# Moving the head transposes of two self-attention blocks into the logits' PSUM slots, and loading weight chunks two ahead

## The chip, the cores and the metric

The kernel runs on one core of a Trainium2 chip. The metric is device time in microseconds (us) of one launch. The kernel before takes 5064.57 us (median of 3 runs, 5062.13 to 5067.9).

## The reference, cut to what matters

A residual stream `x` of 4 batches x 1024 tokens x 288 channels goes through four blocks: a quantised transformer block (0), a cross-attention block (1), a fake-quantised transformer block (2) and a second quantised transformer block (3). The change touches the self-attention of blocks 0 and 3, and the weight preparation that runs beside it:

```python
def quant_linear(q, s, qsum, w, b):        # one scale and zero point per output row of w
    wmax, wmin = jnp.max(w, axis=1), jnp.min(w, axis=1)
    sw = (wmax - wmin) / 255.0 + 1e-08
    zw = _ste_round(-wmin / sw) - 128.0
    qw = jnp.clip(_ste_round(w / sw[:, None]) + zw[:, None], -128.0, 127.0)
    ...
# self-attention: 16 heads of 18 channels, 1024 queries x 1024 keys per batch
logits = jnp.einsum('bqhd,bkhd->bhqk', q, k) / sqrt(18)
o = jnp.einsum('bhqk,bkhd->bqhd', softmax(logits), v)
```

## The kernel before, in words

`quant_net` runs a quantised block: first `quant_self` (self-attention), then cross-attention and the feed-forward part. `quant_self` is called for block 0 (about 55 to 850 us of the profile) and for block 3 (about 3820 to 4600 us); both run the same code.

**The attention loop.** It goes over 4 batches `b`, 4 groups `g` of 4 heads, 2 halves `qh` of 512 queries, and 8 key tiles `kt` of 128 keys: 256 steps a block. A step issues, in program order:

1. logits: two PSUM tiles from `ps2()`, each two banks wide; four matmuls at L2021, one per head, each on its own 32 rows of the array. Heads 0 and 1 write one tile, heads 2 and 3 the other; below these are the two *pairs* of logits. Each matmul is fp32 and appears as two records, so a whole step's logits are "x8" and one pair is "x4";
2. two exponentials on ScalarE (L2031), one per pair, into buffers `e` of the pool `ep`;
3. `weigh` for the step *before*: four matmuls (L1981) that add exp(logits) times values into the accumulator `acc`, a tile from `ps1()`. At the last key tile VectorE copies `acc` to `oT` (L1992). At `kt == 1` of the next head group `turn_heads` calls `heads_done`: four transposes of `oT` on TensorE (L1936), then on VectorE a reciprocal (L1942), a product into the attention output `a` (L1943) and two small reductions (L1953, L1954);
4. `step()`: one piece of side work, if there is any. The list `side` holds the projections of the next group (`operands`, L1896), the next batch's norms and quantisation (`levels`, L1434 and L2358), its values (`values`, L277) and the output projection (`output`, L277). When the list is empty, one piece of `spare` is taken.

**PSUM.** `psum_attn` gives 3 slots of two banks to `ps2()` and 2 slots of one bank to `ps1()`[...]. `acc` holds one `ps1` slot nearly always; the other is shared by every piece of side work and by `heads_done`.

**The order.** Semaphores, slots and each engine's instruction order are set at compile time by a list scheduler: it follows program order as priority, but an engine whose next instruction has no free slot or no data yet, by the scheduler's own estimate, gets a later one that has. [...]

**The weight preparation.** `spare` runs `ctx_aside` and then `ff_aside`, which prepares the two feed-forward weights through `level_pieces`. That loads a chunk of 1152 numbers per partition by a DMA from SyncE's queue (L1545, 432 KB) into a buffer `wn`, reduces it to maxima and minima on VectorE (L1558, L1559), turns these into scales (tile `wps`, 2 buffers), quantises it in 12 pieces (L1583, L1584, L1589), transposes each piece on TensorE (L1599), copies it (L1610) and stores it (L1611). Each of the two feed-forward weights has three chunks, so there are six chunk loads a block. The other weights fit in one chunk each. `wn` has two buffers, and the load of the next chunk is issued when work on a chunk begins.

Of the kernel before, what the change touches and what calls it, by code (L numbers as in the profile page):

```python
# [28 lines left out]
F32 = mybir.dt.float32  # L29
# [7 lines left out]
P = 128  # L37
# [1141 lines left out]
class Fast(Net):  # L1179
# [344 lines left out]
    def level_pieces(self, np_, wd, n_in, width, p, put, sw, bias=None):  # L1524

        nc = self.nc
        oc = wd.shape[0] // p  # L1530
        extra = 0 if bias is None else N_TERMS
        kc = (n_in + extra) // width
        per = max(1, 1152 // n_in)
        run = 3
        if extra:
            bt = np_.tile([p, oc], F32, name="wbias")
            nc.sync.dma_start(bt, bias.rearrange("(c p) -> p c", p=p))
            terms = np_.tile([p, 4, N_TERMS], BF16, name="wterms")
        src = wd.rearrange("(c p) i -> p c i", p=p)

        def load(c0):
            m = min(per, oc - c0)
            wn = np_.tile([P, 1152], F32, tag="wn", name="wn", bufs=2)
            wn = wn[:p, : m * n_in].rearrange("p (c i) -> p c i", c=m)
            nc.sync.dma_start(wn, src[:, c0 : c0 + m, :])  # L1545
            return m, wn

        first = load(0)
        yield
        yield  # L1550
        for c0 in range(0, oc, per):
            m, wn = first
            if c0 + per < oc:
                first = load(c0 + per)
            st = self.sm.tile([P, 6, 4], F32, tag="wps", name="wps", bufs=2)
            mx, mn, rsw, lo, hi = (st[:p, k, :m] for k in range(5))
            s = sw[:, c0 : c0 + m]
            nc.vector.tensor_reduce(mx, wn, AX.X, ALU.max)  # L1558
            nc.vector.tensor_reduce(mn, wn, AX.X, ALU.min)  # L1559
            nc.vector.tensor_tensor(s, mx, mn, ALU.subtract)  # L1560
            nc.vector.tensor_scalar(s, s, 1.0 / 255.0, 1e-8, ALU.mult, ALU.add)
            nc.vector.reciprocal(rsw, s)
            nc.vector.tensor_tensor(lo, mn, rsw, ALU.mult)
            nc.vector.tensor_scalar(lo, lo, -1.0, MAGIC, ALU.mult, ALU.add)
            nc.vector.tensor_scalar(lo, lo, MAGIC, -1.0, ALU.subtract, ALU.mult)
            nc.vector.tensor_scalar(hi, lo, 255.0, None, ALU.add)
            self.watch_range(-256.0, 1.0, lo, "wext")
            if extra:
                d = st[:p, 5, :m]
                nc.gpsimd.tensor_tensor(d, bt[:, c0 : c0 + m], rsw, ALU.mult)  # L1570
                self.three_parts(d, [terms[:, :m, k : k + 1] for k in range(3)])
                for k, n in ((3, 0), (4, 1), (5, 0)):
                    nc.gpsimd.tensor_copy(terms[:, :m, k], terms[:, :m, n])
            yield
            runs = [(c, k0) for c in range(m) for k0 in range(0, kc, run)]
            ahead = None

            for n in range(len(runs) + 1):
                now = ahead
                if n < len(runs):  # L1580
                    c, k0 = runs[n]
                    t = wn[:, c, k0 * width : min((k0 + run) * width, n_in)]
                    nc.vector.tensor_scalar(t, t, rsw[:, c : c + 1], MAGIC, ALU.mult, ALU.add)  # L1583
                    nc.vector.tensor_scalar(  # L1584
                        t, t, MAGIC, lo[:, c : c + 1], ALU.subtract, ALU.max
                    )
                    q = np_.tile([P, run * P], BF16, tag="pq", name="q", bufs=2)
                    q = q[:p, : run * width]
                    nc.vector.tensor_scalar(  # L1589
                        q[:, : run * width - extra], t, hi[:, c : c + 1], None, ALU.min  # L1590
                    )
                    if extra:
                        nc.gpsimd.tensor_copy(q[:, run * width - extra :], terms[:, c, :])
                    ahead = (q, c, k0)
                if now:
                    q, c, k0 = now
                    ps = self.ps1(BF16)
                    for k in range(run):
                        nc.tensor.transpose(  # L1599
                            ps[:width, k * p : (k + 1) * p],  # L1600
                            q[:, k * width : (k + 1) * width],
                            self.idb[:p, :p],
                        )
                    ps = ps[:width, : run * p].rearrange("p (k o) -> p k o", o=p)
                    dst, stored = put(c0 + c)
                    dst = dst[:, k0 : k0 + run, :]
                    if stored:
                        to = np_.tile([P, run * P], BF16, tag="to", name="to", bufs=2)
                        to = to[:width, : run * p].rearrange("p (k o) -> p k o", o=p)
                        nc.vector.tensor_copy(to, ps)  # L1610
                        nc.sync.dma_start(dst, to)  # L1611
                    else:
                        nc.vector.tensor_copy(dst, ps)
                    yield
# [9 lines left out]
    def ctx_aside(self, w, ctxT, mask, cw, np_):  # L1624
# [8 lines left out]
        for b in range(B):  # L1633
            m = np_.tile([P, NTB * T], F32, tag="kv", name="msk")
# [14 lines left out]
        nc.sync.dma_start(cw["swo"].rearrange("(c p) -> p c", p=CK), swo)  # L1649
        kb = cw["kb"]  # L1650
        for g in range(NG):
            wk = np_.tile([P, 1152], F32, tag="wn", name="wn", bufs=2)
            wk = wk[:CK, : NC3 * P].rearrange("p (c o) -> p c o", c=NC3)
            nc.sync.dma_start(
                wk, w["wk2"].rearrange("(c p) o -> p c o", p=CK)[:, :, g * P : (g + 1) * P]
            )
            kg = np_.tile([P, NTB * T], F32, tag="kv", name="kg")
            kg = kg.rearrange("p (b k) -> p b k", b=B)
            nc.gpsimd.memset(kg, 0.0)
            yield  # L1660
            yield
            ps = self.ps1()
            for k in range(NC3):
                nc.tensor.matmul(
                    ps[:, : B * T].rearrange("p (b k) -> p b k", b=B),
                    lhsT=wk[:, k, :],
                    rhs=ctx[:, k, :, 0, :],
                    start=(k == 0),
                    stop=(k == NC3 - 1),
                )  # L1670
            for i in range(4):
                rows = slice(i * HP, (i + 1) * HP)
                nc.vector.tensor_scalar(
                    kg[rows, :, i % 2 * T : (i % 2 + 1) * T],
                    ps[rows, : B * T].rearrange("p (b k) -> p b k", b=B),
                    bk[rows, g : g + 1], None, ALU.add,
                )
            yield

            for pr in range(2):  # L1680
                rows = slice(pr * 64, (pr + 1) * 64)
                ps = self.ps1()
                for b in range(B):
                    nc.tensor.matmul(
                        ps[:, b : b + 1], lhsT=kg[rows, b, :], rhs=bq[rows, g : g + 1],
                        start=True, stop=True,
                    )
                nc.vector.tensor_scalar(
                    kb[:, :, g, pr : pr + 1], ps[:, :B].unsqueeze(2), SCALE, None, ALU.mult
                )  # L1690
                yield
            nc.vector.tensor_scalar(kg, kg, wq["sw"][:, g : g + 1], None, ALU.mult)
            nc.sync.dma_start(cw["kbd"][:, :, g, :], kg)
            yield
        wv = np_.tile([P, 1152], F32, tag="wn", name="wn", bufs=2)
        wv = wv[:CK, : NC3 * C].rearrange("p (c o) -> p c o", c=NC3)
        nc.sync.dma_start(wv, w["wv2"].rearrange("(c p) o -> p c o", p=CK))
        yield
        for b in range(B):
# [4 lines left out]
            ps = self.ps1()  # L1704
# [70 lines left out]
    def quant_self(self, L, w, beside, ready):  # L1775
# [5 lines left out]
        with ExitStack() as es:  # L1781
            pool = lambda name, bufs: es.enter_context(tc.tile_pool(name=name, bufs=bufs))
# [3 lines left out]
            if ready is not None:  # L1786
                wqk = []
                for k in "qk":
                    m = {"T": wp.tile([CK, NC3, NG * P], BF16, name=f"w{k}1T")}
# [6 lines left out]
                wv, wo = (  # L1796
                    self.stored_weight(wp, ready[k], ready[f"s{k}"], w[f"b{k}1"], f"w{k}1")
                    for k in "vo"
                )
            else:  # L1800
                with self.psum8(f"{L}w"), tc.tile_pool(name=f"{L}an", bufs=2) as np_, self.work(f"{L}anw"):
# [7 lines left out]
                        wqk.append(m)  # L1809
                    wv = self.level_weight(wp, np_, [(w["wv1"], w["bv1"])], C, CK, "wv1")  # L1810
                    wo = self.level_weight(wp, np_, [(w["wo1"], w["bo1"])], C, CK, "wo1")
            ep = pool(f"{L}ep", 6)
            es.enter_context(self.work(f"{L}ak"))
            ext = wp.tile([P, 2, 2 * B * NG], F32, name="sext")
            es.enter_context(self.psum_attn(f"{L}x"))
# [115 lines left out]

            def heads_done(b, g, qh, o):

                ps = self.ps1()
                for tt in range(4):
                    nc.tensor.transpose(  # L1936
                        ps[:, tt * P : (tt + 1) * P], o[:, tt * P : (tt + 1) * P], self.idf
# [13 lines left out]
                m = t0 // 4 * NG + g  # L1951
# [1499 lines left out]
```

## Time and profile before

| | |
|---|---|
| median of 3 runs | 5064.57 us |
| span of the profiled execution | 5064.5 us |
| TensorE busy over the span | 4346.0 us (86%) |
| ScalarE busy | 3106.6 us (61%) |
| VectorE busy | 3001.7 us (59%) |
| self-attention loops, TensorE busy | 727.89 of 760 us (block 0), 724.80 of 747 us (block 3) |
| transposes at L1936 | 256, that is 64 groups of four |
| chunk loads at L1545 of feed-forward weights | 12 |

The profile is of one execution. In its timeline a line is: start in us, length in us, engine, line of the kernel, operation, output<-inputs, shapes, number of instructions merged; in brackets the engine's idle time before it and who ended that idle time. "PE" is TensorE's matmuls, "PEld" its weight loads (which overlap matmuls), "DVE" VectorE, "ACT" ScalarE, "POOL" GpSimd, "SPq" SyncE's DMA-issuing queue.

### The profile page before, as it was taken

The page shows a single profiled execution, that of the slowest core. Times are in us where ns is not written, and L with a number is a line of the kernel's source. Part 1 is how long each engine was busy: PE and PEld are TensorE (multiplying, and loading weights), DVE is VectorE, ACT ScalarE, POOL GpSimd, SP SyncE. Part 2 cuts the span into 40 slices and gives each one's busy share as a digit, 9 for nine tenths or more (in the row PEclk, how much of TensorE's full clock was granted, in tenths as well). Part 3 has the DMA queues.
Part 4 walks back from the last instruction along what each step waited for, and adds up shares of the span by engine and source line. Part 5 has one row for each costly group of instructions (what it writes and reads, how often), then busy time and mean ns, then how long its engine had stood idle before and what let it go on. Part 6 is the DMA issues. An engine that isn't in the chain of part 4 may idle for free. (4 is left out here: it accounts for less than half of the span.)

```text
span 5064.5 us, 63950 instructions
## 1 busy us (share of the span) xinstructions
PE 4346.0 (86%) x23291; PEld 1740.0 (34%) x23291; DVE 3001.7 (59%) x6686; ACT 3106.6 (61%) x4374; POOL 1273.7 (25%) x2013
## 2 busy tenths in 40 slices
PE   5999996889898979998798873899998999996786
PEld 2233322545566411100233331455543223322343
DVE  8453253665564679999688778433235444344775
ACT  3776765476663269998788853212215767764796
POOL 1001002442412567200122224111101000003664
PEclk9999997899899955555788785899998999997897
DMA  2000002100001221000000032000000000011000
GB/s 79 3 4 12 7 24 62 60 21 16 1 15 43 112 82 36 11 0 0 23 25 25 22 107 79 23 12 10 1 1 15 7 2 11 15 25 30 16 17 20
DMA packets 135638, 136.00 MB, mean 27 GB/s; under 512 B 69260, under 2 KB 111884, under 8 KB 133648
## 3 DMA queue, kind: packets, MB, share of 16 engines
q1 hardware_dynamic: 134112, 128.13, 8.5%
q0 software_dynamic: 1200, 3.69, 0.3%
q8 instruction: 185, 3.03, 0.3%
q14 instruction: 141, 1.16, 0.1%
HBM read 79.92 MB, written 43.47 MB: 24 GB/s over the span
## 5 line engine op out<-in xcount | busy, mean ns | idle before, releaser
L2031 ACT ACTIVATE e<-ps 128x1024 f32<-128x1024 f32 x1024 | 998.3, 1021 | 467.7 <-PE ps L2021 457.5
L2021 PE MATMUL ps<-qT,kT 32*128 32x512 f32 x4096 | 683.2, 652 | 0.0
L1981 PE MATMUL ps<-e,v 128*32 128x512 f32 x4096 | 560.8, 618 | 15.7 <-DVE oT L1992 15.4
L2940 DVE TENSOR_REDUCE top<-e 128x2 f32<-128x2048 f32 x256 | 561.9, 2272 | 18.6 <-ACT e L2933 18.6
L2933 ACT ACTIVATE e<-ps 128x1024 f32<-128x1024 f32 x512 | 534.5, 1375 | 19.2 <-PE ps L3286 10.9
L3335 ACT ACTIVATE e<-ps 128x1024 f32<-128x1024 f32 x512 | 484.5, 1054 | 90.6 <-PE ps L3326 73.0
L3286 PE MATMUL ps<-qk 32*128 32x512 bf16 x1024 | 511.2, 603 | 24.1 <-ACT e L2933 23.0
L1758 POOL TENSOR_TENSOR x<-x,y 128x288 f32<-128x288 f32 x192 | 153.2, 809 | 873.2 <-DVE y L1757 532.0
L3338 DVE TENSOR_SCALAR eb<-e 128x2048 bf16<-128x2048 f32 x256 | 322.1, 1261 | 50.4 <-ACT e L3335 48.0
L2933 ACT ACTIVATION_READ_ACCUMULATOR e<-ps 128x1 f32 x512 | 283.4, 555 | 0.0
L2021 PEld LDWEIGHTS ps<-qT,kT 32*128 32x128 f32 x4096 | 197.9, 186 | 216.1 <-issue 143.1
L1404 POOL TENSOR_TENSOR h<-h,g 128x288 f32<-128x288 f32 x176 | 141.8, 810 | 499.5 <-ACT h L1401 461.6
L3326 PE MATMUL ps<-qk,kz 64*128 64x512 bf16 x1024 | 226.9, 441 | 45.8 <-ACT e L3335 43.5
L2464 PE MATMUL psf<-hT,w 128*128 128x512 f32 x576 | 258.0, 600 | 0.6 <-ACT hT L2456 0.6
L1981 PEld LDWEIGHTS ps<-e,v 128*32 128x32 f32 x4096 | 81.6, 109 | 414.0 <-issue 350.5
L1349 PE MATMUL ps<-idb,q 128*128 128x128 bf16 (+2 forms) x1152 | 113.8, 244 | 120.2 <-ACT q L1333 69.5
L3286 PEld LDWEIGHTS <-qk 32*128 32x128 bf16 x1024 | 52.6, 99 | 465.3 <-issue 465.3
L3235 ACT ACTIVATE gl<-psf,bf 128x512 f32<-128x512 f32 x72 | 46.0, 684 | 270.1 <-PE psf L2468 265.8
L1354 ACT COPY qT<-ps 98x384 bf16<-98x384 bf16 (+3 forms) x256 | 151.8, 642 | 73.3 <-PE ps L1349 73.2
L1880 POOL TENSOR_TENSOR v<-y,wv1b 128x288 f32<-128x288 f32 x64 | 51.3, 806 | 516.2 <-DVE y L1877 516.2
L3239 DVE SCALAR_TENSOR_TENSOR u<-psf,bf,gl 128x512 f32<-128x512 f32 x72 | 51.1, 746 | 217.0 <-ACT gl L3235 217.0
L277 PEld LDWEIGHTS <-qT 98*128 98x128 bf16 (+2 forms) x1344 | 135.5, 105 | 126.8 <-issue 41.5
(487 smaller groups left out, 7826.6 us busy)
## 6 DMA issues: line engine op xcount, KB each, us to landing
raw<-y SPq DMA_DIRECT2D x32, 432.0 KB
in<-raw SPq DMA_DIRECT2D x32, 432.0 KB
kz<-qk SPq DMA_DIRECT2D x128, 64.0 KB
wn<-in_L_wfc SPq DMA_DIRECT2D x12, 432.0 KB
x<-in_x SPq DMA_DIRECT2D x4, 1152.0 KB
vvo<-vt SPq DMA_DIRECT2D x16, 288.0 KB
vo<-vvo SPq DMA_DIRECT2D x4, 1152.0 KB
rawq<-y SPq DMA_DIRECT2D x32, 144.0 KB
```

The costliest lines, as they stand in the source:

```text
L1354: nc.scalar.copy(qT[:, c0 : c0 + r, j0 * P : (j0 + per) * P].rearrange("p c (a t) -> p a c t", a=per), ps[:width, : per * r * P].rearrange ...
L1758: nc.gpsimd.tensor_tensor(self.x[:, t, :], self.x[:, t, :], y, ALU.add)
L1981: nc.tensor.matmul(acc[i * HP : (i + 1) * HP, :], lhsT=st["v"][:, kt, h * (D + 1) : h * (D + 1) + HP], rhs=es_[i // 2][:, i % 2, :], start ...
L2021: nc.tensor.matmul(pss[i // 2][:, i % 2, :], lhsT=self.row_tile(kT, i)[:, kt * P : (kt + 1) * P], rhs=self.row_tile(qT, i)[:, qh * 512 : ( ...
L2031: nc.scalar.activation(e, ps, AF.Exp, scale=SCALE)
L2464: nc.tensor.matmul(o, lhsT=lhs(i)[:, c, :], rhs=rhs(i)[:, c, :], start=(c == 0), stop=False)
L2933: nc.scalar.activation(e[:, j, :].rearrange("p (a n) -> p a n", a=2), sc, AF.Exp, scale=rstep, accum_out=sums[:, t, h0 + j : h0 + j + 1],)
L2940: nc.vector.tensor_reduce(top[:, t, h0 : h0 + 2], e, AX.X, ALU.max)
L3286: self.nc.tensor.matmul(ps[:, c, :], lhsT=self.row_tile(qT, i)[:, g, qt * P : (qt + 1) * P], rhs=self.row_tile(kT, i)[:, g, c * 512 : (c + ...
L3326: nc.tensor.matmul(pss[i][:, n, :], lhsT=kz[rows, i, kt * P : (kt + 1) * P], rhs=qT[rows, g, qh * 512 : (qh + 1) * 512], start=True, stop= ...
L3335: nc.scalar.activation(e[:, 2 * n : 2 * n + 2, :], ps, AF.Exp, scale=step)
L3338: nc.vector.tensor_scalar(eb, e, MAGIC, MAGIC, ALU.add, ALU.subtract)
```

## The change

Three things change.

- `heads_done` takes its PSUM tile from `ps2()` (the first bank of a two-bank slot of the logits) and no longer from `ps1()`.
- `level_pieces` loads its first two chunks at the start and then chunk c+2 when work on chunk c begins; the buffers `wn` are three, also where `ctx_aside` uses them.
- The pool `ep` of exponentials has five buffers where it had six.

```diff
         def load(c0):
             m = min(per, oc - c0)
-            wn = np_.tile([P, 1152], F32, tag="wn", name="wn", bufs=2)
+            wn = np_.tile([P, 1152], F32, tag="wn", name="wn", bufs=3)
             ...
-        first = load(0)
+        loaded = [load(c0) for c0 in range(0, oc, per)[:2]]
         yield
         yield
         for c0 in range(0, oc, per):
-            m, wn = first
-            if c0 + per < oc:
-                first = load(c0 + per)
+            m, wn = loaded.pop(0)
+            if c0 + 2 * per < oc:
+                loaded.append(load(c0 + 2 * per))
...
-            wk = np_.tile([P, 1152], F32, tag="wn", name="wn", bufs=2)
+            wk = np_.tile([P, 1152], F32, tag="wn", name="wn", bufs=3)
...
-        wv = np_.tile([P, 1152], F32, tag="wn", name="wn", bufs=2)
+        wv = np_.tile([P, 1152], F32, tag="wn", name="wn", bufs=3)
...
-            ep = pool(f"{L}ep", 6)
+            ep = pool(f"{L}ep", 5)
...
             def heads_done(b, g, qh, o):
 
-                ps = self.ps1()
+                ps = self.ps2()[:, 0, :]
                 for tt in range(4):
                     nc.tensor.transpose(
```

## The prediction

> **What bounds it now.** I read the page first, for the lines of the loop, then the table of stages for the two self-attention loops, then the timeline of TensorE round all 64 head transposes, and last the timeline of the weight chunks.
>
> ```profile
> L2031 ACT ACTIVATE e<-ps 128x1024 f32<-128x1024 f32 x1024 | 998.3, 1021 | 467.7 <-PE ps L2021 457.5
> L1981 PE MATMUL ps<-e,v 128*32 128x512 f32 x4096 | 560.8, 618 | 15.7 <-DVE oT L1992 15.4
> ```
> ```profile
> 75.00:835.00 760.00, 727.89 (x4950) 216.91 (x4948) 333.23 (x987) 518.11 (x548) 57.38 (x107) 0.98 0.04 11
> 3840.00:4587.00 747.00, 724.80 (x4966) 216.74 (x4963) 323.20 (x914) 518.12 (x548) 56.92 (x106) 0.97 0.04 10
> ```
>
> ScalarE's exponentials are idle 467.7 us ahead of their work, almost all of it waiting for logits; TensorE hardly waits. In the stages (columns: TensorE, its weight loads, VectorE, ScalarE, GpSimd busy, then granted clock) TensorE is busy 728 of 760 and 725 of 747 us at a clock of 0.98. So these loops are bound by the order of TensorE's queue: an instruction that leaves it shortens the kernel. After the loops the next phase needs their last output, so a gain there isn't swallowed.
>
> The timeline shows an ordinary step with side work and then a step with head transposes:
>
> ```profile
> 187.64 0.82 PE L1896 MATMUL ps<-hT,wq1T 96*128 96x512 bf16 x3
> ...
> 188.40 1.14 PE L2021 MATMUL ps<-qT,kT 32*128 32x512 f32 x8
> ...
> 189.47 1.06 PE L1981 MATMUL ps<-e,v 128*32 128x512 f32 x8
> 189.63 1.94 ACT L2031 ACTIVATE e<-ps 128x1024 f32<-128x1024 f32 x2 [0.88 <-PE ps L2021]
> ...
> 190.46 0.66 PE L1936 MATMUL ps<-idf,oT 128*128 128x128 f32 x4
> ...
> 191.05 1.13 PE L2021 MATMUL ps<-qT,kT 32*128 32x512 f32 x4
> ...
> 191.45 0.46 DVE L1943 TENSOR_TENSOR a<-ps,rc 128x288 f32<-128x288 f32 x1
> ...
> 192.11 0.82 PE L1896 MATMUL ps<-hT,wk1T 96*128 96x512 bf16 x3
> ...
> 192.86 1.13 PE L2021 MATMUL ps<-qT,kT 32*128 32x512 f32 x4
> ...
> 193.92 1.06 PE L1981 MATMUL ps<-e,v 128*32 128x512 f32 x8
> ```
>
> In the ordinary step the four logits go together (x8) in 1.14 us. In the head step they are torn apart: one pair (x4), the side work L1896, the other pair, each pair 1.13 us. The reason is in the program: `acc` and the transposes hold both `ps1` slots, so L1896 had to be placed after VectorE's read of the transposes, and the first pair was put ahead of it.
>
> For the weights:
>
> ```profile
> 711.40 1.26 SPq L1545 DMA_DIRECT2D wn<-in_L_wfc  x1
> ```
> ```profile
> 716.12 1.35 DVE L1558 TENSOR_REDUCE wps<-wn 96x4 f32<-96x1152 f32 x1 [5.41 <-DMA wn<-in_L_wfc]
> ...
> 717.73 0.29 PE L1599 MATMUL ps<-idb,q 96*98 96x96 bf16 x3 [3.25 <-DVE to L1610]
> ```
> ```profile
> 781.32 0.42 PE L1599 MATMUL ps<-idb,q 96*128 96x96 bf16 x3 [4.58 <-DVE a L1943]
> ...
> 781.67 1.94 PE L1981 MATMUL ps<-e,v 128*32 128x512 f32 x8
> ```
>
> VectorE stands 5.41 us at the head of its list until a chunk lands that was only requested when the last buffer fell free; TensorE then stands 3.25 us. At 781 us the same costs 4.58 us, and the value products after it take 1.94 us, not 1.06.
>
> [...] The trace's issue-to-reduction time of 4.7 us (711.40 to 716.12) is used.
>
> **The transposes in a logits slot.** Transposes, reciprocal and product stay as they are; only the slot moves. Going through all 64 groups in TensorE's timeline, 52 have the torn pattern: 28 with L1896, 12 with L277, 4 each with L2358 and L1599, 2 each with L1434 and L1684. Two more keep their logits together but wait for `a` (4.58 and 3.98 us), eight have no side work or (the first) a wait of their own, two close a block. In a torn step the next value products start 3.45 us after the transposes with L1896 and 3.17 with L277. From rows of ordinary steps, untorn it would be transposes 0.59, L1896 0.75 (L277: 0.47), logits 1.07: 2.41 (2.13). The difference is 1.04 us both times: 52 x 1.04 = 54 us.
>
> Does the third slot carry it? Take the transposes as time 0. The previous logits fill two slots, whose exponentials run from -0.83 to +1.11 (189.63 + 1.94). The transposes take the third, and VectorE has read it at +1.45. The next logits come at 0.59 + 0.75 = 1.34: both older slots are free by then, and the step after, at about +4.2, finds the borrowed one free too. ScalarE needs 2.04 us a step against 3.4 now taken. Where there is no side work (8 steps), the second pair comes at 1.1 and not 0.59; that is up to 0.5 us each, 4 us, but ScalarE paces these steps (two exponentials 2.04 us, steps 2.07 to 2.37), so between 0 and 4: I take 2. Two steps with L2358 also show TensorE waiting 1.81 us for VectorE's L1954, behind which the slot is freed; VectorE is late there for other reasons too, so 0 to 3.6: I take 2. Sum 54, bounds 45 to 58.
>
> **Weights two ahead.** The 12 feed-forward chunks make VectorE wait 38.0 us, every one of them. The load still waits for the same event (the buffer of chunk c-1), at the same place of SyncE's queue, so the stores behind it there wait no longer than before; but its reduction is now due a chunk later. GpSimd's small copies follow VectorE. TensorE's idle time that comes from these waits, with the stretch of half clock after it: block 0, at 717.73, 747.41 and 781.32 us, 3.25 + 3.20 + 4.58 idle, plus 4.9 of slow products; block 3, at 4469, 4499 and 4532, 2.63 + 3.39 + 3.98 plus 6.0. That makes 21.0 + 10.9 = 32 us. Two reductions of 1.35 us and some fifteen small operations stay on VectorE and can still hold up `oT` or `to`: I leave 4. On the other side, the first two chunks now arrive together (at about 457 and 4211 us). VectorE already delays `oT` there by 2.99 and 2.85 us, having drawn the first chunk's reductions forward; the second chunk may join them, at up to 2.7 us of reductions and a second landing, say 5 a block: 0 to 10, I take 3. Sum 25, bounds 5 to 33. The shorter waits for the single-chunk weights are taken as nothing: their products lie on TensorE's list by priority, and I saw no TensorE wait for them.
>
> **Five `e` buffers** cost nothing: when a step's exponentials write two, the only others alive are the two of the step before, since TensorE runs every product of the step before that ahead of these logits. That makes four. If this cover failed, ScalarE would wait for L1981 about as long as a pair of products; a handful would be below 5 us.
>
> The sum is 79 us from a span of 5064.5 us, which equals the median of 5064.57 to within its spread: about 4986 us, bounds 4966 to 5014.
>
> **Rivals.** The list is made at compile time, so the change may not do what it says.
> - *Only the weights gain.* The scheduler still finds something to put between the pairs, because it thinks the second pair's slot is not yet free. For it: a head step now needs both older slots, an ordinary one only the first. Against: the side work comes between and gives 0.75 us. 5064.5 - 25 = 5040.
> - *Only the heads gain.* VectorE's list draws reductions forward as soon as data is thought to be there, so waits move and do not vanish, and the bunching at 457 us costs its 10: 5064.5 - 54 + 8 = about 5019.
> - *Slower: the borrowed slot starves the logits.* With one slot gone, the pairs wait for their exponentials one at a time; as soon as the first exponential is done, two of the four value products are ready and get placed between the pairs. Then the logits stay torn and the values are torn too, 0.99 us more in each of some 62 steps: +61 - 25 = about 5100. It decides from the point where the scheduler has the second exponential end later than the first pair of logits. On the chip it ends 0.23 us before the logits begin, and on steps without side work 0.5 us after; that speaks against it, but only the scheduler's times count.
>
> **The numbers.** The forecast has 0.70, "only weights" 0.08, "only heads" 0.09, slower 0.09; 0.04 is left for gains and losses that cancel. A measurement of this kernel can tell about 0.2% (10 us) from no change. Faster by more than that: 0.87; within: 0.04; slower: 0.09. The range 4964 to 5040 takes in the forecast's bounds, "only heads" and "only weights", and leaves out the slower case.
>
> **What would show it.** In the profile after: head steps read transposes, side work, logits x8, values, about 2.4 us from transposes to values; TensorE's matmul busy time in each loop falls by some 27 us; no VectorE reduction L1558 of chunks 3 to 6 waits for a DMA, and the 4.58 and 3.98 us gaps are gone. Wrong would be: logits in x4 pieces after transposes, value products in x4 pieces, ScalarE waiting for L1981, or an `oT` wait at 460 us that has grown beyond 6 us.

## The result, and the profile after

The changed kernel takes 4969.52 us (median of 4 runs), the kernel before in the same comparison 5063.35: a ratio of 0.9823, 95% interval [0.9807, 0.9838]. The profiled execution has a span of 4966.1 us, against 5064.5. A second set of executions (e9 below) gave 0.9819 [0.9805, 0.9832]. Every ratio is of executions in the usual fast state; the one that was not, at 7432.35 us in e7 below, is left out.

First the page's groups, the two lines that answer to those shown of before:

```profile
L2031 ACT ACTIVATE e<-ps 128x1024 f32<-128x1024 f32 x1024 | 992.6, 1021 | 382.1 <-PE ps L2021 370.9
...
L1981 PE MATMUL ps<-e,v 128*32 128x512 f32 x4096 | 550.5, 608 | 12.4 <-DVE oT L1992 12.4
```

The exponentials wait for logits 370.9 us and no longer 457.5. That is 86.6 us less, most of the 98.4 us by which the span fell, and logits remain the only thing that they wait for. Then the timeline of a head step, the same one (same projection L1896) as before:

```profile
185.08 0.66 PE L1936 MATMUL ps<-idf,oT 128*128 128x128 f32 x4
...
185.58 0.81 PE L1896 MATMUL ps<-hT,wk1T 96*128 96x512 bf16 x3
...
186.07 0.46 DVE L1943 TENSOR_TENSOR a<-ps,rc 128x288 f32<-128x288 f32 x1
186.32 0.31 PEld L2021 LDWEIGHTS ps<-qT,kT 32*128 32x128 f32 x8 [0.42 <-ACT e L2031]
186.32 1.14 PE L2021 MATMUL ps<-qT,kT 32*128 32x512 f32 x8
...
187.39 1.06 PE L1981 MATMUL ps<-e,v 128*32 128x512 f32 x8
```

Side work follows the transposes at once, the logits are whole again (x8), and from transposes to value products it is 2.31 us where it was 3.46 (190.46 to 193.92). No head step of either block is torn any more. The weight load of the logits now names ScalarE (`ACT e L2031`) as what it waited for, since the logits need the slots of both older exponentials.

For the weights, the view of line L1558 (what VectorE waited for ahead of the chunk reductions: us, times) and two of its lines in the timeline:

```profile
  DMA wn<-in_L_wfc: 6.1, 4
```
```profile
422.30 1.35 DVE L1558 TENSOR_REDUCE wps<-wn 96x4 f32<-96x1152 f32 x1 [1.75 <-DMA wn<-in_L_wfc]
...
680.91 1.35 DVE L1558 TENSOR_REDUCE wps<-wn 96x4 f32<-96x1152 f32 x1
```

The waits fell from 38.0 us in 12 places to 6.1 in 4: only each block's first two chunks still wait. The third chunk, which waited 5.41 us, starts at once. (A chunk is quantised in four pieces, in the second weight in three, and not in 12 as written above: 12 chunks have 42 stores at L1611.)

Adding up TensorE's timeline from one set of value products to the next, in steps of three kinds (two blocks together), shows where the time came from. A head step is one with head transposes:

| | 62 head steps | 320 steps with side work | loops, first logits to last transposes |
|---|---|---|---|
| before | 277.6 us | 908.1 us | 760.4 + 745.2 us |
| heads only (e1) | 213.0 | 904.1 | 723.8 + 711.5 |
| weights only (e2) | 279.5 | 890.8 | 750.9 + 740.4 |
| changed kernel | 204.1 | 883.2 | 704.1 + 700.5 |

In a second profile of the changed kernel (e9) each of these sums agrees within about 2 us. The time between the two loops differs by 9 us between these two profiles, so small effects are better read in the loops.

### The profile page after: what moved, and what is told of

The parts are those of the page before. It is cut to its first block, busy times and chain, and to the rows that moved or that the text cites. A ratio compares the mean times of both kernels' runs of the same rounds, so it can differ in the third digit from the quotient of the medians.

```text
span 4966.1 us, 63954 instructions
## 1 busy us (share of the span) xinstructions
PE 4252.1 (86%) x23291; PEld 1719.8 (35%) x23291; DVE 3001.3 (60%) x6686; ACT 3097.4 (62%) x4374; POOL 1273.1 (26%) x2013
## 5 line engine op out<-in xcount | busy, mean ns | idle before, releaser
L2031 ACT ACTIVATE e<-ps 128x1024 f32<-128x1024 f32 x1024 | 992.6, 1021 | 382.1 <-PE ps L2021 370.9
L2021 PE MATMUL ps<-qT,kT 32*128 32x512 f32 x4096 | 625.3, 644 | 3.9 <-DVE a L1943 3.7
L1981 PE MATMUL ps<-e,v 128*32 128x512 f32 x4096 | 550.5, 608 | 12.4 <-DVE oT L1992 12.4
L2933 ACT ACTIVATE e<-ps 128x1024 f32<-128x1024 f32 x512 | 534.0, 1369 | 19.5 <-PE ps L3286 10.9
L277 PEld LDWEIGHTS <-qT 98*128 98x128 bf16 (+2 forms) x1344 | 133.4, 103 | 128.3 <-issue 44.5
```

The costliest lines, as they stand in the source:

```text
L1981: nc.tensor.matmul(acc[i * HP : (i + 1) * HP, :], lhsT=st["v"][:, kt, h * (D + 1) : h * (D + 1) + HP], rhs=es_[i // 2][:, i % 2, :], start ...
L2021: nc.tensor.matmul(pss[i // 2][:, i % 2, :], lhsT=self.row_tile(kT, i)[:, kt * P : (kt + 1) * P], rhs=self.row_tile(qT, i)[:, qh * 512 : ( ...
L2031: nc.scalar.activation(e, ps, AF.Exp, scale=SCALE)
L2933: nc.scalar.activation(e[:, j, :].rearrange("p (a n) -> p a n", a=2), sc, AF.Exp, scale=rstep, accum_out=sums[:, t, h0 + j : h0 + j + 1],)
```

## The experiments

Theory A is the prediction's: two gains that add. The rivals were that one half carries everything (B), or that the halves pay only together (C). Each ratio is to the kernel before, on the same chip.

**e1, heads only.**

```diff
# kernel before
-                ps = self.ps1()
+                ps = self.ps2()[:, 0, :]
```

> Only the slot of the head transposes changes (ps2 instead of ps1); two wn buffers, one chunk ahead and six e buffers stay. Theory A (two separate gains, as the prediction summed them): the torn head steps close up, 52 x 1.0 to 1.15 us, minus about 3 us where no side work fills the step; loss of the two long waits for a slot (4.58 and 3.98 us) partly comes with it: about 5003 us, 5000 to 5012. Rival B (the gain is the reshuffled VectorE list that three wn buffers bring, and the slot matters little): above 5040 us. In the profile A expects head steps of 2.2 to 2.4 us from transposes to value products and the VectorE waits for wn unchanged near 38 us.

Measured: 4992.69 us, ratio 0.9863 [0.9839, 0.9886], some 69 us. No head step is torn, and the VectorE waits for `wn` are 38.7 us as before. The slot alone brings three quarters of the gain, more than A had expected. Rival B does not hold.

**e2, weights only.**

```diff
# changed kernel
-                ps = self.ps2()[:, 0, :]
+                ps = self.ps1()
```

> Only the weights change: three wn buffers, two chunks ahead, five e buffers; the head transposes stay in ps1. Theory A: VectorE waits for feed-forward chunks fall from 38 to about 6 to 8 us, TensorE's gaps near 717, 747 and 781 us and their counterparts in block 3 go: 25 to 35 us, so 5030 to 5040 us; head steps stay torn (x4, side work, x4; 3.45 us). Rival B: 4990 us or less. Rival C (the two parts only pay together, since a torn step hides the wait): 5055 us or more.

Measured: 5059.79 us, ratio 0.9998 [0.9988, 1.0009]: nothing. A is missed, and the time is the one that rival C gave. Yet VectorE's waits for the feed-forward chunks did fall to 6.0 us, and steps with side work did get 17.3 us shorter, so C's reason, that a torn step hides the wait, does not explain it. Two head steps ate 11.5 of the 17.3 us. They are the ones with L1684 in batch 1, 3.68 us each from transposes to values before; here they take 9.41 and 9.27. The first of them before:

```profile
444.79 0.66 PE L1936 MATMUL ps<-idf,oT 128*128 128x128 f32 x4
...
448.47 1.06 PE L1981 MATMUL ps<-e,v 128*32 128x512 f32 x8
```

And here:

```profile
442.08 0.31 SPq L1545 DMA_DIRECT2D wn<-in_L_wfc  x1
...
445.83 1.35 DVE L1558 TENSOR_REDUCE wps<-wn 96x4 f32<-96x1152 f32 x1 [1.72 <-DMA wn<-in_L_wfc]
...
447.43 0.66 PE L1936 MATMUL ps<-idf,oT 128*128 128x128 f32 x4
448.02 1.13 PE L2021 MATMUL ps<-qT,kT 32*128 32x512 f32 x4
...
452.48 0.44 DVE L1943 TENSOR_TENSOR a<-ps,rc 128x288 f32<-128x288 f32 x1
...
453.06 1.84 PE L1684 MATMUL ps<-csm,kg 64*128 64x1 f32 x8 [3.92 <-DVE sext L1954]
454.83 2.08 PE L2021 MATMUL ps<-qT,kT 32*128 32x512 f32 x4
...
456.84 1.94 PE L1981 MATMUL ps<-e,v 128*32 128x512 f32 x8
```

With a third buffer free, the block's first chunk is requested at 442 us and not at 457, ahead of this head step where it was behind it. Its reductions and scales fill VectorE from 445.83 on, so L1943 reads the transposes only at 452.48. The transposes hold the shared `ps1` slot until then, and TensorE stands 3.92 us before L1684; then its matmuls take nearly twice as long (2.08 and 1.94 us, where 1.14 and 1.06 are usual). This became theory D: the earlier transfer meets the shared slot. The second step is the same place in block 3.

**e3, five `e` buffers alone.**

```diff
# kernel before
-            ep = pool(f"{L}ep", 6)
+            ep = pool(f"{L}ep", 5)
```

> Only the pool of exponentials shrinks from six buffers to five. Theory A: nothing, within 5 us of before, as TensorE's list is the same and only four buffers are ever alive at once. Rival: the missing buffer lets ScalarE wait for value products, up to 1 us in each head step: 10 to 60 us slower, with L1981 named as what ScalarE waits for.

Measured: 5063.46 us, ratio 1.0003 [0.9995, 1.0011]. Nothing, as A had it.

**e4, three buffers but one chunk ahead.**

```diff
# weights-only kernel
-        loaded = [load(c0) for c0 in range(0, oc, per)[:2]]
+        loaded = [load(0)]
...
-            if c0 + 2 * per < oc:
-                loaded.append(load(c0 + 2 * per))
+            if c0 + per < oc:
+                loaded.append(load(c0 + per))
```

> Three wn buffers and five e buffers, but the chunk loads are issued only one ahead as before; heads in ps1. Theory A2 (the third buffer is what frees the load, since before it each load stood waiting for the last buffer): the load of a chunk no longer waits for a buffer, so it lands long before use: the same time as with two ahead, 5030 to 5042 us, VectorE waits for wn under 10 us. Rival (issuing two ahead is what counts): 5055 us or more, with VectorE waits near 38 us.

Measured: 5059.97 us, ratio 1.0000 [0.9989, 1.0011], VectorE's waits for chunks 6.1 us. The time expected was wrong, as for e2. But the waits fall just as with two ahead: the third buffer frees the loads, not the place in the program from which they are issued.

**e5, the borrowed slot for 2 of the 64 head transposes.**

```diff
# weights-only kernel
-                ps = self.ps1()
+                ps = self.ps2()[:, 0, :] if (b, g, qh) == (1, 3, 0) else self.ps1()
```

> The weights-only kernel (three wn, two ahead, five e), with the borrowed slot for just 2 of the 64 head transposes: those of batch 1, group 3, first half, in each block. There the weights-only trace shows L1684 waiting 3.9 us for L1954 and the step taking 9.4 and 9.3 us, against 3.7 before the change. Theory D (the earlier chunk load draws VectorE's reductions into this one head step, where TensorE stands behind the shared slot, and that eats the weights' gain): both steps fall to about 2.6 to 4.5 us, 10 to 14 us faster than weights only: about 5047 us, 0.2 to 0.35% below before. Rival (the weights' gain is lost elsewhere): 2 us faster than weights only, as two steps are worth 1.04 us each.

Measured: 5050.96 us, ratio 0.9966 [0.9953, 0.9979]; weights only had 0.9998. TensorE's list differs from the weights-only kernel in just those two steps, and they now take 2.63 and 2.64 us. The timeline of the first:

```profile
438.59 1.35 DVE L1558 TENSOR_REDUCE wps<-wn 96x4 f32<-96x1152 f32 x1 [1.77 <-DMA wn<-in_L_wfc]
...
439.99 0.66 PE L1936 MATMUL ps<-idf,oT 128*128 128x128 f32 x4
440.57 1.05 PE L1684 MATMUL ps<-csm,kg 64*128 64x1 f32 x8
441.55 1.14 PE L2021 MATMUL ps<-qT,kT 32*128 32x512 f32 x8
...
445.16 0.46 DVE L1943 TENSOR_TENSOR a<-ps,rc 128x288 f32<-128x288 f32 x1
445.76 1.14 PE L2021 MATMUL ps<-qT,kT 32*128 32x512 f32 x8 [2.07 <-DVE a L1943]
```

VectorE is as late as before, L1943 coming 5.2 us after the transposes. But what it holds up is now a slot of the logits that is needed one step later: 2.07 us of waiting for 3.92. The ratio moved by 0.32%, about 16 us, a little more than the 10 to 14 that D expected, where the rival had 2. The two steps themselves account for 13.5 us from values to values. D stands: two steps of 512 hid most of the gain from the weights.

**e6, heads and five `e` buffers.** The e1 kernel with the edit of e3.

> The borrowed slot for all head transposes and five e buffers, but two wn buffers and one chunk ahead. It separates what is left between heads only (4993 us) and the whole change (4970 us). Theory D: the buffers of e give nothing and the weights all of the 23 us: 4988 to 4996 us. Rival (five e buffers, by another order of VectorE's list at the start of block 0, where the five-e run lost 9 us before the loop and won 15 in it, carry part): 4975 to 4986 us.

Measured: 4996.04 us, ratio 0.9865 [0.9851, 0.9879], the same as e1. So beside the borrowed slot the weights are worth 0.9865 - 0.9823 = 0.42%, about 21 us, and the `e` buffers nothing. The gain lies in the steps with side work: 903.8 us here, 883.2 in the changed kernel.

**e7, no side work in head steps.**

```diff
# kernel before; weigh() returns whether it turned heads
-                            if len(late) > 1:
-                                weigh(*late.pop(0))
-                            step()
+                            turned = len(late) > 1 and weigh(*late.pop(0))
+                            if not turned:
+                                step()
```

> The kernel before, with the head transposes still in ps1, but no piece of side work is taken in a head step; it is taken in a later step. Theory A (the logits are torn because side work and transposes want the same slot): no step is torn, a head step takes 1.65 us from transposes to values and not 3.45, and each displaced piece costs 0.3 to 0.6 us in a step that had none: 52 x (1.8 - 0.5) = 40 to 70 us faster, 4995 to 5025 us. Rival (tearing comes from the logits' three slots being too few in a head step, whoever holds the other two): head steps stay in x4 pieces, within 10 us of before.

Measured: 5033.88 us (median of five), ratio 0.9928 [0.9915, 0.9941], some 36 us: less than expected. A head step, from the timeline of TensorE (the logits are L2023 in this kernel):

```profile
182.95 0.66 PE L1936 MATMUL ps<-idf,oT 128*128 128x128 f32 x4
183.54 1.14 PE L2023 MATMUL ps<-qT,kT 32*128 32x512 f32 x8
184.61 1.07 PE L1981 MATMUL ps<-e,v 128*32 128x512 f32 x8
```

With the transposes still in `ps1`, no head step is torn: 1.66 us. So it is side work and transposes wanting one slot that tears the logits, not the number of the logits' slots. The gain is smaller because the displaced pieces cost more than the 0.3 to 0.6 us reckoned. In block 0, head steps fall by 51 us, steps without side work by 25 (12 fewer of them), and steps with side work rise by 47; 47 - 25 over 31 pieces is 0.7 us each. Nearly half of that lies in two steps of each block, where the kernel empties the list `side` ahead of the last head group of a batch. Four pieces with L277 meet in one step, and the logits go one head at a time:

```profile
384.35 0.54 PE L277 MATMUL ps<-wv1T,hT 96*128 96x288 bf16 x3
384.82 1.12 PE L2023 MATMUL ps<-qT,kT 32*128 32x512 f32 x2
385.88 0.54 PE L277 MATMUL ps<-wv1T,hT 96*128 96x288 bf16 x3
```

These four steps take 7.6 to 8.4 us from values to values, where an ordinary step with L277 takes 2.54. Without these steps a displaced piece costs 0.4 to 0.5 us, as expected. One head's logits take as long here (1.12 us) as four together (1.14).

**e8, head transposes after the next logits.**

```diff
# changed kernel: moved from weigh() to behind the logits of the loop
-                if done and kt == 1:
-                    turn_heads()
...
+                            if done and kt == 2:
+                                turn_heads()
```

> The changed kernel, with the head transposes issued one place later: after the next step's logits and before the value products. Theory E (head steps with little side work now stand at 2.22 us because the second pair of logits waits for the slot of the second older exponential, which ends 1.1 us after the transposes begin): the logits then need only one older slot, the steps with L277, L1599, L2358, L1434 fall by about 0.1 us and those without side work by up to 0.55: 3 to 10 us faster than the changed kernel, 4960 to 4967 us. Rival (the borrowed slot is missed one step later instead): equal or slower, 4970 to 4990 us, with value products or logits in x4 pieces.

Measured: 4975.99 us, ratio 0.9812 [0.98, 0.9825], not to be told from the changed kernel. Most steps did what E said. From values to values, with L1599 2.89 us for 3.22, with L277 3.13 for 3.21, without side work 2.89 for 3.21; but those with L1896 went from 3.30 to 3.41, one of them to 5.99, and two with L277 took 4.8. The head steps' sum rose from 204.1 to 209.1 us, and the loops by 6.

**e9, the changed kernel again**, as the measure for the next two.

> The changed kernel itself, as the measure for the two runs beside it: about 4970 us, 0.981 to 0.984 of before.

Measured: 4974.64 us, ratio 0.9819 [0.9805, 0.9832].

**e10, the place chosen by the side work.**

```diff
# changed kernel; the old place stays for projections
+                            if done and kt == 2 and not (side and side[0].__name__ == "operands"):
+                                turn_heads()
```

> The changed kernel, with the head transposes issued after the next logits unless the side work of that step is a projection (L1896), in which case they stay where the change put them. From the two places measured, values to values: steps with L277 3.13 against 3.21 us, with L1599 2.89 against 3.22, without side work 2.89 against 3.21, with L1896 3.30 kept. 12 x 0.08 + 6 x 0.33 + 8 x 0.32 = 5.5 us faster than the changed kernel. Rival (the moved place also moves the output projection by a step, and the order of everything after it): within 5 us to either side, not to be told from the changed kernel.

Measured: 4976.43 us, ratio 0.9823 [0.981, 0.9837]. The rival's answer: L1896 steps are back at 3.30 us, L1599 steps at 2.89, yet the head steps' sum is 204.5 us, the changed kernel's 204.1. Two steps with L277 now take 4.8 us.

**e11, one buffer for the scales.**

```diff
# changed kernel
-            st = self.sm.tile([P, 6, 4], F32, tag="wps", name="wps", bufs=2)
+            st = self.sm.tile([P, 6, 4], F32, tag="wps", name="wps", bufs=1)
```

> The changed kernel with one buffer for the scales (wps) where there are two, so that no chunk's reductions can stand on VectorE's list before the chunk ahead of it is done. Theory D (what is left of the weights' cost is VectorE's bunched reductions: oT late by 3.3, 3.1 and twice 1.5 us, each with a stretch of half clock): 3 to 10 us faster than the changed kernel if the bunching comes from the second buffer. Rival (the scales then come late for TensorE's transposes L1599, once per chunk): six times 2 to 4 us a block slower, 10 to 40 us above the changed kernel.

Measured: 4970.62 us, ratio 0.9812 [0.9799, 0.9826], 4 us below e9 with intervals that overlap. In the trace the waits of 3.3 and 3.1 us for `oT`, where the second chunk's reductions had been drawn forward, are gone, and TensorE meets two new ones of 0.84 and 0.7 us per block for L1599. So the second buffer is the cause of these two waits, as D had it. Those of 1.5 us for `oT` stay, and behind them the products take 1.06 or 1.07 us and the logits 1.14, as usual, in either trace. The two loops together are 6 us shorter than in e9, which fits D, but the size is not settled by one trace and times that overlap.

No kernel here is shown to be faster than the changed one.

## Why the prediction was right, point by point

- **What bounds it.** Right: TensorE's queue in the two loops. The loops fell by 101 us. Outside them about 9 us came back before block 0's first logits (74.7 to 84.0 us), which the five-`e` run e3 shows too, with the loop of block 0 15 us shorter there and the time the same. Some 6 us went between the loops, less than the two profiles of the changed kernel differ there.
- **The sum and its bounds.** The forecast of 79 us is 94 between the medians, and the time of 4969.52 us lies near the lower end of the range. The bounds of the two parts, 45 to 58 and 5 to 33, add up to 50 to 91 us, that is 4973 to 5014 us; the prediction wrote 4966. So the measured time lies just outside the sum of its own parts, and it is partly luck that the range took it in.
- **Torn logits.** The mechanism was right and e7 and e1 show it. The size was low: 54 us forecast, bounds 45 to 58, and some 69 measured (e1). In the 52 torn steps it was close: 56 us forecast with the 2 for L2358, 59.9 measured in e1. The step with L1896 came to 2.30 us, not 2.41, because the transposes take 0.50 us ahead of a bf16 projection and 0.59 ahead of logits. The step with L277 came to 2.22, not 2.13, because the second pair waits for the older exponential. These errors cancel: over the 48 steps without L2358 the gain is 1.05 us each, and 1.04 was forecast. The four with L2358 gained 9.6 us together, since the two that waited for VectorE's L1954 no longer do.
- **A wait booked in one column that belongs to both.** Most of the rest of e1's surplus is in the two waits for L1943 at 781 and 4532 us, which were booked as the weights' gain. In e1 both steps fell to 3.22 us from 7.66 and 7.05 (values to values), though the slot is all that changed; in e2 they were still 7.25 and 6.34. Part of the wait came back beside them in e1: 2.01 us at 746 us, 1.08 and 2.29 us at 4461 and 4473, for the copies at L1610. So a late VectorE and the shared slot made this wait together.
- **Half clock.** The prediction booked 10.9 us of slow products after six waits. The granted clock was 0.50 for 78.5 us of the two loops before (12 stretches of 3.41 to 10.24 us) and for 30.7 after (five). The products after the 4.58 us gap at 781 us, in a stretch at 0.50, took 1.94 us for 1.06, 1.83 times as long; if that holds for all of this time, the difference is worth an estimated 22 us. This is part of the gains above, and no single run separates it. It shows in TensorE's busy time, which was to fall by some 27 us in each loop and fell by 39 and 37 (to 689.33 and 687.55 us).
- **Steps without side work.** Forecast to lose 0 to 0.5 us each, 2 in all; they stand at 3.21 us where they were 2.66, and lost 3.5 us in e1.
- **The weights.** 25 us forecast, about 21 us measured beside the borrowed slot (e6 against the changed kernel), but nothing alone (e2). The agreement is partly luck, since 8.6 us of the idle time behind the 25 belong to the slot as well. The step that failed is the one that let the two sums stand independently. It took the first load to stay at 457 us, with the second chunk arriving beside it, and looked at `oT` for the cost: 3 us of a bound of 10. In the changed kernel the first two chunks are requested at 418.5 and 439.1 us, and the waits for `oT` hardly grew (3.31 and 3.07 us). The real place was a head step 15 us earlier, where L1684 stood behind the shared slot: 11.5 us in two steps of e2. The whole change escapes most of it, because the borrowed slot gives VectorE one more step of time. So the sum held for the two edits together, and "only the weights gain, 5040 us" would have been wrong for the weights alone.
- **Five `e` buffers.** Nothing, as forecast (e3, e6). TensorE's order in e3 is that of before; the orders of VectorE, ScalarE and GpSimd are not.
- **Slower rival.** Nothing of it was seen: no value products in x4 pieces. The borrowed slot did starve the logits in one step per block, by 2.05 and 1.67 us, where VectorE is late.

The 94 us between the medians are then some 69 for the heads (forecast 54) and 21 for the weights (25), to within the intervals.

## What to carry to other kernels

Where one pool serves a long-lived accumulator and everything else, look at what the scheduler puts into the wait for its last slot. Here it split a pack of four matmuls that run together. Each half took as long as the whole pack (1.13 us for 1.14), and the loss showed up as busy time, not as idle time. A prefetch that removes its wait can be worth nothing until the place it moves work into can bear a late reader; price an earlier transfer where its consumer will now run, and try two edits apart and together before adding their gains.

## What the runs showed of the hardware that was not expected

TensorE ran at half speed after gaps shorter than the six of 2.63 to 4.58 us behind which the prediction had booked slow products. In the changed kernel a gap of 2.05 us, a few microseconds after 1 us of one-column matmuls (L1684), was followed by products of 1.93 us in place of 1.06, at a granted clock of 0.50 from 430.6 to 434.0 us:

```profile
429.47 1.14 PE L2021 MATMUL ps<-qT,kT 32*128 32x512 f32 x8 [2.05 <-DVE a L1943]
430.54 1.93 PE L1981 MATMUL ps<-e,v 128*32 128x512 f32 x8
```

The length of the gap does not decide it alone. In e5 the same gap of 1.81 us stands ahead of the same work in both blocks, with no L1684 near. In block 3 logits then take 2.08 us, in block 0 the usual 1.13:

```profile
4094.02 1.19 PE L2358 MATMUL ps<-idf,scol 128*128 128x128 f32 x4 [1.81 <-DVE sext L1954]
4095.15 2.08 PE L2021 MATMUL ps<-qT,kT 32*128 32x512 f32 x4
```
```profile
346.74 0.68 PE L2358 MATMUL ps<-idf,scol 128*128 128x128 f32 x4 [1.81 <-DVE sext L1954]
347.35 1.13 PE L2021 MATMUL ps<-qT,kT 32*128 32x512 f32 x4
```

The kernel before has the same pair. Behind the 1.81 us that end at 4102.35 us the granted clock was 0.50 up to 4108.9 us and the logits took 2.08 us; behind the 1.81 us that end at 351.55 us it stayed at 1.00 and they took 1.13. What decides between the two is not shown.
